# Two attention layers on one TensorE: score, value and sum matmuls as 64x64 quadrants, with part of the row sums on GpSimd

## Chip, core and metric

The kernel runs on one core of a Trainium2 chip. The metric is the time of one execution on the device, in microseconds. The core's engines are TensorE (PE in the profile; its weight loads are listed apart as PEld), VectorE (DVE), ScalarE (ACT), GpSimd (POOL) and SyncE (SP). Everything is computed in float32.

## What is computed

The reference is a chain of four attention-like layers on a tensor of 2 x 512 x 32 x 32. Layer 0 is a deformable attention with a small network for its bias, layer 1 a linear attention. Layers 2 and 3 are plain softmax attentions with 8 heads of 64 channels over 1024 positions, each with a group norm ahead of it and a residual behind it. Only those two are touched here. Cut to its core, layer 2 is (layer 3 differs in the group norm and in the order of the weights only):

```python
xn = group_norm(x)                                              # (2, 512, 1024)
q, k, v = split(einsum('oc,bcn->bon', qkv_w, xn) + qkv_b)       # 8 heads of 64 channels each
attn = softmax(einsum('bhcn,bhcm->bhnm', q, k) * 64 ** -0.5)    # over the keys m
out = einsum('bhnm,bhcm->bhcn', attn, v)
return einsum('oc,bcn->bon', proj_w, out) + proj_b + residual
```

## The kernel before

Layers 0 and 1 come first and take three quarters of the time. Then `attention` (L646) runs for layer 2 and for layer 3: it computes queries, keys and values (`queries_keys_values`, L671), branches on whether all logits are small enough to do without subtracting a maximum, runs `heads_bounded` (L783) in the branch that these inputs take, and projects the result (`project`, L423).

A query or key tile holds two heads: partitions 0 to 63 are the channels of one (par 0), 64 to 127 those of the other (par 1). `heads_bounded` goes over 16 units a layer, 32 in all: 2 batches b, 4 head pairs p, 2 halves h of 512 queries. A unit has eight blocks n of 128 keys. For each block

- `score` (L797) makes logits with the keys on the partitions: for each of the two heads a matmul with 64 rows (channels) and 128 columns (keys) over 512 queries (L804), into a PSUM tile s of 128 x 2 x 512. ACT takes the exponential into the SBUF tile e (L812), and DVE adds e to a running sum over the blocks (L816 for the first two blocks, L818 after that: seven additions a unit);
- `value` (L820) multiplies by the values: for each head a matmul with 128 rows (keys) and 64 columns (channels), accumulated over the eight blocks in a PSUM tile o of 128 x 512 (L829).

After the eighth block, a matmul with a matrix of ones, again 128 rows and 64 columns for each head (L840), adds the sum over its partitions into a PSUM tile d; DVE takes the reciprocal (L842) and multiplies o by it (L843). The result overwrites the query tile, which is no longer needed.

The order of PE's instructions is written by hand (`manual_schedule`, L847): two blocks of scores, then the two blocks of values of the step before, and so on across units. Other engines take their instructions in program order, each waiting by semaphores for its inputs and for buffers to come free. A float32 matmul shows as two records in the trace, each with a weight load of its own and one pass over the 512 columns.

[...] Here s has two buffers of two banks, o two of one bank, d two of one bank: all eight. In SBUF there are six e buffers and two each for the sum and for the reciprocal r.

Before and behind the heads: the last value projections (L739), and `project_one` (L429), which needs all four tiles of a batch, batch 0 first.

Of the kernel before, what the change touches and what calls it, by code (L numbers as in the profile page):

```python
# [11 lines left out]
F32 = mybir.dt.float32  # L12
AF = mybir.ActivationFunctionType
ALU = mybir.AluOpType
# [4 lines left out]
P = 128  # L19
# [3 lines left out]
NB = N // P  # L23
HF = 512
DH = 64
# [22 lines left out]
class Net:  # L48
# [734 lines left out]
    def heads_bounded(self, k, ones, data):  # L783

        nc = self.nc
        with ExitStack() as ctx:  # L790
            ep = self.pool(ctx, f"b{k}_e", 6)
            ap = self.pool(ctx, f"b{k}_a", 2)
            ps_s = self.pool(ctx, f"b{k}_ps_s", 2, psum=True)
            ps_o = self.pool(ctx, f"b{k}_ps_o", 2, psum=True)
            ps_d = self.pool(ctx, f"b{k}_ps_d", 2, psum=True)

            def score(unit, n):  # L797
                b, p, h, state = unit
                qs, ks, _ = data[b]
                cut = slice(h * HF, (h + 1) * HF)  # L800
                s = ps_s.tile([P, 2, HF], F32, tag="s", name=f"s{k}{b}{p}{h}{n}")
                for par in range(2):
                    rows = slice(par * DH, (par + 1) * DH)
                    nc.tensor.matmul(  # L804
                        s[:, par, :],
                        lhsT=ks[p][rows, n * P : (n + 1) * P],
                        rhs=qs[p][rows, cut],
                        start=True,
                        stop=True,
                    )  # L810
                e = ep.tile([P, 2, HF], F32, tag="e", name=f"e{k}{b}{p}{h}{n}")
                nc.scalar.activation(e, s, AF.Exp)  # L812
                state.setdefault("e", {})[n] = e
                if n == 1:
                    state["sum"] = ap.tile([P, 2, HF], F32, tag="sum", name=f"sum{k}{b}{p}{h}")
                    nc.vector.tensor_tensor(state["sum"], state["e"][0], e, ALU.add)  # L816
                elif n > 1:
                    nc.vector.tensor_tensor(state["sum"], state["sum"], e, ALU.add)  # L818

            def value(unit, n):  # L820
                b, p, h, state = unit
                v = data[b][2]
                if n == 0:
                    state["o"] = ps_o.tile([P, HF], F32, tag="o", name=f"o{k}{b}{p}{h}")
                e = state["e"].pop(n)
                for par in range(2):
                    rows = slice(par * DH, (par + 1) * DH)
                    at = (2 * p + par) * DH
                    nc.tensor.matmul(  # L829
                        state["o"][rows, :],  # L830
                        lhsT=v[:, n, at : at + DH],
                        rhs=e[:, par, :],
                        start=(n == 0),
                        stop=(n == NB - 1),
                    )
                if n == NB - 1:
                    d = ps_d.tile([P, HF], F32, tag="d", name=f"d{k}{b}{p}{h}")
                    for par in range(2):
                        rows = slice(par * DH, (par + 1) * DH)
                        nc.tensor.matmul(d[rows, :], lhsT=ones, rhs=state["sum"][:, par, :], start=True, stop=True)  # L840
                    r = ap.tile([P, HF], F32, tag="r", name=f"r{k}{b}{p}{h}")
                    nc.vector.reciprocal(r, d)  # L842
                    nc.vector.tensor_tensor(data[b][0][p][:, h * HF : (h + 1) * HF], state["o"], r, ALU.mult)  # L843

            units = [(b, p, h, {}) for b in range(B) for p in range(CT) for h in range(2)]
            steps = [(unit, n) for unit in units for n in range(NB)]
            with self.tc.manual_schedule(engines={mybir.EngineType.PE}):  # L847
                for i in range(0, len(steps) + 2, 2):
                    for unit, n in steps[i : i + 2]:
                        score(unit, n)  # L850
                    if i >= 2:
                        for unit, n in steps[i - 2 : i]:
                            value(unit, n)

    def heads_general(self, k, data):
        with ExitStack() as ctx:
# [196 lines left out]
```

## Time and profile before

| | us |
|---|---|
| median of 3 runs (4030.8 to 4035.1) | 4033.99 |
| the profiled execution, its own time | 4034.45 |
| its span in the trace | 4032.7 |
| PE busy in the span | 3924.8 (97%) |
| first score matmul of layer 2 to the start of its last d matmul | 3217.10 to 3473.77 |
| first score matmul of layer 3 | 3711.08 |

Times in the trace count from the start of the span. "Busy" of PE is the time in which at least one matmul is under way by the records; the ends of matmuls are modelled, so starts are the surer numbers. In the lists of groups a line names the source line, the engine, the operation, the tiles written and read, the shapes and the count; then the busy time in us, the mean duration of one in ns, and the idle time of the engine before such instructions with what ended it. In the view in order of time a line has start and length in us, both over a run of merged records, then engine, line, operation, tiles and count.

The DVE instructions of the heads last 1.21 us for an addition of 1024 columns, 3.36 for the reciprocal and 0.68 for the final product; an exponential on ACT lasts 1.02. POOL does nothing in the heads.

### The profile page before, as it was taken

The numbers are of one execution on the slowest core, as the hardware profiler recorded it, in microseconds if no ns is written. First come the engines' busy times: TensorE is split into PE (matmuls) and PEld (weight loads), VectorE is DVE, ScalarE is ACT, GpSimd is POOL, SyncE is SP. The second block draws the span as 40 slices with busy tenths as digits, with TensorE's granted clock in tenths as the row PEclk, the third lists the DMA queues.
The fourth block names the chain that finished last, engine by engine and source line by source line (L and its number), as shares of the span: only waits on it lengthen the run. The fifth ranks groups of instructions, "written<-read, shape, count | busy, mean of one in ns | idle before, by whom it ended". The sixth has DMA issues, their size and how long they took to land.

```text
span 4032.7 us, 34844 instructions
## 1 busy us (share of the span) xinstructions
PE 3924.8 (97%) x13792; PEld 1541.1 (38%) x13792; DVE 2264.8 (56%) x2484; ACT 1793.3 (44%) x1778; POOL 69.5 (2%) x78
## 2 busy tenths in 40 slices
PE   6999999999999999999999999999999999999999
PEld 2333333333333333333333333444464433343333
DVE  7766766766766567766766654000024277633774
ACT  5656655655655456665665553111101144211441
POOL 0000000000000000000000000000001100011000
PEclk9999999999999999999999999999999999999999
DMA  1000000000000000000000002100000000000001
GB/s 63 1 1 0 1 1 1 1 0 1 1 1 1 1 1 1 1 1 1 1 1 17 1 1 84 42 0 0 0 1 3 32 1 1 2 13 0 1 1 43
DMA packets 7521, 31.91 MB, mean 8 GB/s; under 512 B 945, under 2 KB 1457, under 8 KB 6065
## 3 DMA queue, kind: packets, MB, share of 16 engines
q1 hardware_dynamic: 6624, 27.46, 1.8%
q8 instruction: 116, 1.90, 0.2%
q10 hardware_dynamic: 720, 2.05, 0.1%
q14 instruction: 61, 0.49, 0.0%
HBM read 25.32 MB, written 4.19 MB: 7 GB/s over the span
## 4 chain that ended last, share of the span: by engine, by line
PE 91%; DVE 4%; ACT 4%; issue 0%; POOL 0%; DMA 0%; ACTq 0%; DVEq 0%
PE hp L356 41%; PE sim L325 10%; PE s L804 6%; PE o L829 6%; PE m L469 5%; PE m L478 5%; PE qk0p L698 3%; PE pb L435 3%; PE qk1p L698 3%; PE vp L739 2%; PE out_b L435 1%; DVE h L344 1%; DVE conv L203 1%; ACT h L358 1%; ACT L304 1%; ACT log L304 1%
## 5 line engine op out<-in xcount | busy, mean ns | idle before, releaser
L356 PE MATMUL hp<-h,w 128*128 128x512 f32 x4096 | 1840.3, 600 | 45.4 <-ACT h L358 34.0
L344 DVE CUSTOM_DVE_ANT_1 h<-t 128x1024 f32<-128x1024 f32 x1024 | 1249.4, 1223 | 637.0 <-PE hp L356 636.5
L358 ACT ACTIVATE h<-hp,cols 128x1024 f32<-128x1024 f32 x1024 | 1137.4, 1113 | 875.6 <-PE hp L356 870.0
L356 PEld LDWEIGHTS hp<-h,w 128*128 128x128 f32 x4096 | 750.2, 190 | 1085.2 <-issue 670.4
L325 PE MATMUL sim<-h,w 128*32 128x512 f32 x4096 | 489.7, 598 | 0.0
L812 ACT ACTIVATE e<-s 128x1024 f32<-128x1024 f32 x256 | 248.2, 1022 | 255.4 <-PE s L804 255.4
L804 PE MATMUL s<-q,k 64*128 64x512 f32 x1024 | 254.5, 615 | 5.1 <-ACT e L812 3.4
L818 DVE TENSOR_TENSOR sum<-sum,e 128x1024 f32<-128x1024 f32 x192 | 233.0, 1214 | 41.4 <-ACT e L812 30.9
L829 PE MATMUL o<-e,v 128*64 128x512 f32 x1024 | 247.5, 605 | 0.0
L325 PEld LDWEIGHTS sim<-h,w 128*32 128x32 f32 x4096 | 108.4, 109 | 343.9 <-issue 343.9
L469 PE MATMUL m<-mx,w 128*128 128x512 f32 x512 | 221.6, 594 | 0.7 <-ACT att L420 0.7
L478 PE MATMUL m<-mh,w 128*128 128x512 f32 x512 | 220.4, 592 | 0.0
L473 ACT ACTIVATE mh<-m,cols 128x512 f32<-128x512 f32 x64 | 44.0, 688 | 336.5 <-PE m L469 336.5
L486 DVE SCALAR_TENSOR_TENSOR x<-m,cols,x 128x512 f32<-128x512 f32 x16 | 12.0, 751 | 318.0 <-PE m L478 318.0
L804 PEld LDWEIGHTS s<-q,k 64*128 64x128 f32 x1024 | 88.1, 186 | 169.4 <-issue 86.9
L469 PEld LDWEIGHTS m<-mx,w 128*128 128x128 f32 x512 | 97.4, 190 | 124.3 <-issue 122.0
L478 PEld LDWEIGHTS m<-mh,w 128*128 128x128 f32 x512 | 97.3, 190 | 122.5 <-issue 122.5
L710 ACT ACTIVATE k<-qk1p,cols 128x512 f32<-128x512 f32 x32 | 22.0, 687 | 245.0 <-PE qk1p L698 245.0
L829 PEld LDWEIGHTS o<-e,v 128*64 128x64 f32 x1024 | 62.2, 136 | 169.8 <-issue 169.2
L698 PE MATMUL qk0p<-xn,qkv 128*128 128x512 f32 x256 | 118.1, 615 | 3.2 <-ACT xn L779 3.2
L435 PE MATMUL pb<-q,proj 128*128 128x512 f32 x256 | 112.2, 600 | 5.3 <-issue 5.3
L842 DVE RECIPROCAL r<-d 128x512 f32<-128x512 f32 x32 | 107.4, 3358 | 15.0 <-PE d L840 15.0
(165 smaller groups left out, 1999.9 us busy)
## 6 DMA issues: line engine op xcount, KB each, us to landing
w<-in_mlp_w SPq DMA_DIRECT2D x8, 1024.0 KB, 11.8
qkv<-in_l_qkv SPq DMA_DIRECT2D x8, 768.0 KB, 6.6
x<-in_x SPq DMA_DIRECT2D x8, 512.0 KB, 8.0
out<-x SPq DMA_DIRECT2D x8, 512.0 KB, 2.6
proj<-in_l_proj SPq DMA_DIRECT2D x8, 256.0 KB, 6.2
l1w<-in_l_w SPq DMA_DIRECT2D x1, 1280.0 KB, 5.4
ow<-in_out_w ACTq DMA_DIRECT2D x1, 1024.0 KB, 12.2
qkv<-in_l_qkv ACTq DMA_DIRECT2D x1, 768.0 KB, 8.2
```

The costliest lines, as they stand in the source:

```text
L325: nc.tensor.matmul(sim[at : at + 32, :], lhsT=self.l0w3[:, 31 - s : 63 - s], rhs=h2[jj][:, h * HF : (h + 1) * HF], start=(s == 0), stop=False,
L344: nc.vector._custom_dve(TENSOR_ADD_SAT, out=h1, in0=t[:, 0, j, :].unsqueeze(1).to_broadcast([P, H, W]), in1=t[:, 1, j, :].unsqueeze(2).to_ ...
L356: nc.tensor.matmul(hp[:, cut], lhsT=self.l0w2, rhs=flat[:, cut], start=True, stop=True)
L358: nc.scalar.activation(y, hp, AF.Relu, bias=self.col("cpb_b2"))
L435: nc.tensor.matmul(acc, lhsT=wt[:, o * P : (o + 1) * P], rhs=att[t][:, cut], start=(t == 0), stop=(t == CT - 1))
L469: nc.tensor.matmul(acc, lhsT=w1[t][:, o * P : (o + 1) * P], rhs=xn[t], start=(t == 0), stop=(t == CT - 1))
L478: nc.tensor.matmul(acc, lhsT=w2[t // 4][:, t % 4, o * P : (o + 1) * P], rhs=hs[t], start=(t == 0), stop=(t == nh - 1),)
L698: nc.tensor.matmul(acc, lhsT=qkv[c][:, at : at + P], rhs=xn[c][:, cut], start=(c == 0), stop=(c == CT - 1),)
L804: nc.tensor.matmul(s[:, par, :], lhsT=ks[p][rows, n * P : (n + 1) * P], rhs=qs[p][rows, cut], start=True, stop=True,)
L812: nc.scalar.activation(e, s, AF.Exp)
L818: nc.vector.tensor_tensor(state["sum"], state["sum"], e, ALU.add)
L829: nc.tensor.matmul(state["o"][rows, :], lhsT=v[:, n, at : at + DH], rhs=e[:, par, :], start=(n == 0), stop=(n == NB - 1),)
```

## The change

Only `heads_bounded` changes.

- Scores: each head's matmul is cut into two, of 64 keys each, so that a block has four matmuls of 64 rows and 64 columns, one in each quadrant of the array. The tile s is the same as before.
- Values: each head's matmul is cut by rows into two of 64 keys each. The two halves of the keys accumulate apart, in two banks of o (o[:, 0] and o[:, 1]), which are added at the end: ACT copies o[:, 0] to the result tile (the former query tile), and DVE adds o[:, 1] to it there.
- Sums: the matmul with ones is cut in the same way, with two banks of d. ACT copies one to t, DVE adds the other, takes the reciprocal in place and multiplies the result tile by it. This is now a function of its own, `divide`.
- The row sums: blocks 0, 1, 3 and 5 are added by GpSimd (three additions, tile some), blocks 2, 4, 6 and 7 by DVE (three additions, tile sum), and DVE adds the two (one more).
- The order on PE: one block of scores, one block of values (two blocks behind), and `divide` two blocks after the last values of its unit.
- Buffers: o and d have one buffer of two banks each instead of two of one bank; some and t (tag r) have one, sum two.

Besides what the diff shows, the built program has this order for DVE within a unit: the sum of blocks 2 and 4, the product that ends the unit before, blocks 6 and 7, the addition of some, the addition of o[:, 1], that of d[:, 1], the reciprocal. On ACT the copy of o stands between the exponentials of the next unit's blocks 1 and 2, the copy of d between those of blocks 3 and 4. The first value matmul of a unit waits for the DVE addition of o[:, 1] of the unit before. The first sum of a unit on POOL waits for the addition of some of the unit before.

```diff
+        halves = [slice(0, DH), slice(DH, P)]
...
-            ap = self.pool(ctx, f"b{k}_a", 2)
+            ap = self.pool(ctx, f"b{k}_a", 1)
+            ap2 = self.pool(ctx, f"b{k}_a2", 2)
             ps_s = self.pool(ctx, f"b{k}_ps_s", 2, psum=True)
-            ps_o = self.pool(ctx, f"b{k}_ps_o", 2, psum=True)
-            ps_d = self.pool(ctx, f"b{k}_ps_d", 2, psum=True)
+            ps_o = self.pool(ctx, f"b{k}_ps_o", 1, psum=True)
...
-                for par in range(2):
-                    rows = slice(par * DH, (par + 1) * DH)
-                    nc.tensor.matmul(
-                        s[:, par, :],
-                        lhsT=ks[p][rows, n * P : (n + 1) * P],
-                        rhs=qs[p][rows, cut],
-                        start=True,
-                        stop=True,
-                    )
+                for par, rows in enumerate(halves):
+                    for c in range(2):
+                        at = n * P + c * DH
+                        nc.tensor.matmul(
+                            s[halves[c], par, :], lhsT=ks[p][rows, at : at + DH], rhs=qs[p][rows, cut], start=True, stop=True
+                        )
...
                 if n == 1:
-                    state["sum"] = ap.tile([P, 2, HF], F32, tag="sum", name=f"sum{k}{b}{p}{h}")
-                    nc.vector.tensor_tensor(state["sum"], state["e"][0], e, ALU.add)
-                elif n > 1:
+                    state["some"] = ap.tile([P, 2, HF], F32, tag="some", name=f"some{k}{b}{p}{h}")
+                    nc.gpsimd.tensor_tensor(state["some"], es[0], e, ALU.add)
+                elif n in (3, 5):
+                    nc.gpsimd.tensor_tensor(state["some"], state["some"], e, ALU.add)
+                elif n == 4:
+                    state["sum"] = ap2.tile([P, 2, HF], F32, tag="sum", name=f"sum{k}{b}{p}{h}")
+                    nc.vector.tensor_tensor(state["sum"], es[2], e, ALU.add)
+                elif n in (6, 7):
                     nc.vector.tensor_tensor(state["sum"], state["sum"], e, ALU.add)
+                if n == NB - 1:
+                    nc.vector.tensor_tensor(state["sum"], state["sum"], state["some"], ALU.add)
...
-                    state["o"] = ps_o.tile([P, HF], F32, tag="o", name=f"o{k}{b}{p}{h}")
...
+                    state["o"] = ps_o.tile([P, 2, HF], F32, tag="o", name=f"o{k}{b}{p}{h}")
+                o, e = state["o"], state["e"][n]
+                for r, rows in enumerate(halves):
+                    for par in range(2):
+                        at = (2 * p + par) * DH
+                        nc.tensor.matmul(
+                            o[halves[par], r, :],
+                            lhsT=v[rows, n, at : at + DH],
+                            rhs=e[rows, par, :],
+                            start=(n == 0),
+                            stop=(n == NB - 1),
+                        )
                 if n == NB - 1:
...
+                    res = data[b][0][p][:, h * HF : (h + 1) * HF]
+                    nc.scalar.copy(res, o[:, 0, :])
+                    nc.vector.tensor_tensor(res, o[:, 1, :], res, ALU.add)
+
+            def divide(unit):
+                b, p, h, state = unit
+                d = ps_o.tile([P, 2, HF], F32, tag="d", name=f"d{k}{b}{p}{h}")
+                for r, rows in enumerate(halves):
                     for par in range(2):
...
+                        nc.tensor.matmul(
+                            d[halves[par], r, :], lhsT=ones[rows, :], rhs=state["sum"][rows, par, :], start=True, stop=True
+                        )
+                t = ap.tile([P, HF], F32, tag="r", name=f"r{k}{b}{p}{h}")
+                nc.scalar.copy(t, d[:, 0, :])
+                nc.vector.tensor_tensor(t, d[:, 1, :], t, ALU.add)
+                nc.vector.reciprocal(t, t)
+                res = data[b][0][p][:, h * HF : (h + 1) * HF]
+                nc.vector.tensor_tensor(res, res, t, ALU.mult)
...
-                for i in range(0, len(steps) + 2, 2):
-                    for unit, n in steps[i : i + 2]:
-                        score(unit, n)
-                    if i >= 2:
-                        for unit, n in steps[i - 2 : i]:
-                            value(unit, n)
+                for i in range(len(steps) + 4):
+                    if i < len(steps):
+                        score(*steps[i])
+                    if 2 <= i < len(steps) + 2:
+                        value(*steps[i - 2])
+                    if i >= 4 and steps[i - 4][1] == NB - 1:
+                        divide(steps[i - 4][0])
```

More of the change, by code (lines that the diff above doesn't have):

```diff
@@ L801, in score @@
                 s = ps_s.tile([P, 2, HF], F32, tag="s", name=f"s{k}{b}{p}{h}{n}")
-                for par in range(2):
-                    rows = slice(par * DH, (par + 1) * DH)
-                    nc.tensor.matmul(
-                        s[:, par, :],
-                        lhsT=ks[p][rows, n * P : (n + 1) * P],
-                        rhs=qs[p][rows, cut],
-                        start=True,
-                        stop=True,
-                    )
+                for par, rows in enumerate(halves):
[4 more added lines that the diff above has]
+                        )
                 e = ep.tile([P, 2, HF], F32, tag="e", name=f"e{k}{b}{p}{h}{n}")
                 nc.scalar.activation(e, s, AF.Exp)
-                state.setdefault("e", {})[n] = e
+                es = state.setdefault("e", {})
+                es[n] = e
                 if n == 1:
-                    state["sum"] = ap.tile([P, 2, HF], F32, tag="sum", name=f"sum{k}{b}{p}{h}")
-                    nc.vector.tensor_tensor(state["sum"], state["e"][0], e, ALU.add)
-                elif n > 1:
+                    state["some"] = ap.tile([P, 2, HF], F32, tag="some", name=f"some{k}{b}{p}{h}")
[6 more added lines that the diff above has]
+                elif n in (6, 7):
                     nc.vector.tensor_tensor(state["sum"], state["sum"], e, ALU.add)
+                if n == NB - 1:
+                    nc.vector.tensor_tensor(state["sum"], state["sum"], state["some"], ALU.add)
             def value(unit, n):
@@ L823, in value @@
                 if n == 0:
-                    state["o"] = ps_o.tile([P, HF], F32, tag="o", name=f"o{k}{b}{p}{h}")
[L825 to L835, printed above, removed]
@@ L836, in value @@
-                if n == NB - 1:
-                    d = ps_d.tile([P, HF], F32, tag="d", name=f"d{k}{b}{p}{h}")
-                    for par in range(2):
[L839 to L843, printed above, removed]
+                    state["o"] = ps_o.tile([P, 2, HF], F32, tag="o", name=f"o{k}{b}{p}{h}")
```

## The prediction

> **What bounds the kernel now.** I read the page first, then the busy times of the two stretches that the change touches, then one period of them in order of time, then single lines for durations.
>
> ```profile
> PE 3924.8 (97%) x13792; PEld 1541.1 (38%) x13792; DVE 2264.8 (56%) x2484; ACT 1793.3 (44%) x1778; POOL 69.5 (2%) x78
> ...
> PE 91%; DVE 4%; ACT 4%; issue 0%; POOL 0%; DMA 0%; ACTq 0%; DVEq 0%
> ...
> L812 ACT ACTIVATE e<-s 128x1024 f32<-128x1024 f32 x256 | 248.2, 1022 | 255.4 <-PE s L804 255.4
> L804 PE MATMUL s<-q,k 64*128 64x512 f32 x1024 | 254.5, 615 | 5.1 <-ACT e L812 3.4
> L818 DVE TENSOR_TENSOR sum<-sum,e 128x1024 f32<-128x1024 f32 x192 | 233.0, 1214 | 41.4 <-ACT e L812 30.9
> L829 PE MATMUL o<-e,v 128*64 128x512 f32 x1024 | 247.5, 605 | 0.0
> ...
> L842 DVE RECIPROCAL r<-d 128x512 f32<-128x512 f32 x32 | 107.4, 3358 | 15.0 <-PE d L840 15.0
> ```
>
> PE carries the chain. Each f32 matmul has two records (1024 records, 512 calls). ACT waits for scores; PE hardly waits for ACT. The two head stretches, by engine:
>
> ```profile
> 3217.00:3480.00 263.00, 258.40 (x1093) 80.80 (x1094) 196.95 (x144) 126.69 (x130) 0.00 (x0) 1.00 0.03 10
> 3711.00:3976.00 265.00, 260.85 (x1096) 81.87 (x1097) 196.96 (x144) 125.40 (x129) 0.00 (x0) 0.99 0.00 1
> ```
>
> Columns: length, then PE, weight loads, DVE, ACT, POOL. So PE bounds these 528 us; DVE has 25% to spare, ACT half. One period (two key blocks) in order of time, weight loads marking the starts of passes:
>
> ```profile
> 3272.60 0.30 PEld L804 LDWEIGHTS s<-q,k 64*128 64x128 f32 x4 [0.81 <-ACT e L812]
> 3272.60 1.99 PE L804 MATMUL s<-q,k 64*128 64x512 f32 x8
> 3273.14 0.19 PEld L804 LDWEIGHTS s<-q,k 64*128 64x128 f32 x2 [0.23 <-issue]
> 3273.57 0.19 PEld L804 LDWEIGHTS s<-q,k 64*128 64x128 f32 x2 [0.23 <-issue]
> ...
> 3274.52 0.20 PEld L829 LDWEIGHTS o<-e,v 128*64 128x64 f32 x4 [0.76 <-issue]
> ...
> 3275.00 0.14 PEld L829 LDWEIGHTS o<-e,v 128*64 128x64 f32 x2 [0.28 <-issue]
> 3275.43 0.14 PEld L829 LDWEIGHTS o<-e,v 128*64 128x64 f32 x2 [0.29 <-issue]
> 3276.39 0.29 PEld L804 LDWEIGHTS s<-q,k 64*128 64x128 f32 x3 [0.81 <-ACT e L812]
> ```
>
> A pass (two matmuls side by side) starts 0.43 us after the last one (3273.14 to 3273.57; 0.4293 over 27 steps of the L478 stream). Around a change of shape it is longer: 0.54 and 0.48 after the first pass, and 0.52 to 0.53 before it. The period is 3276.39 - 3272.60 = 3.79 = 8 x 0.429 + 0.35: **0.35 us per period is the price of two changes of shape.** A unit (four periods and the d passes) takes 16.00 (d starts at 3251.86 and 3267.86).
>
> **What the Trainium skill says.** (1) "TensorEngine Tiling (Array Packing)", Key Properties: changing the tiling mode, not just the tile, drains TensorE. The trace agrees: 0.35 us per two changes. (2) "TensorE: Matmul & The Clock Gate", Part 3: a weight load overlaps running matmuls only if its row group differs. The trace disagrees: full-height loads (0.19 us) in the L478 stream leave passes at 0.43. (3) "SBUF — State Buffer", Who interferes with whom: a DVE instruction with two SBUF inputs and a GpSimd instruction reading SBUF hold a port in turn; the later one blocks. No run here shows it: no such pair overlaps in the trace of before.
>
> **The change, part by part.** *Quadrants.* A block of scores becomes four 64x64 matmuls, and so do the values: still two passes of 512 columns per stage, 2 x 0.429 = 0.858 us, if four run at once. Four at once is shown for column tiles: L325's 16 records take 1.92 us a visit (4 passes plus one change), with passes 0.43 apart. All three stages have one shape now, so I cost a boundary at nothing: loads of the next stage lie under the pass before, as between consecutive score blocks. PE per unit: 17 x 0.858 = **14.59** against 16.00, 1.41 less. This is a gain on the path.
>
> *One o buffer.* o was double; now the next unit's first value matmul waits until o is emptied by an ACT copy and then a DVE add. Let the last value stage start at 0. Its second pass starts at 0.43 and, with a row's 0.59, ends at 1.02. ACT took up the exponential of the preceding score block at 0.21 and, at the 0.92 spacing of back-to-back ones, is free at 1.13. The copy takes 0.58 (L195, 128x512), to 1.71; the add 0.68 (L843's form), from 1.75 to 2.43. PE has one score block to do meanwhile, to 1.72, and then waits. Behind the waiting matmul stand all later scores, so ACT starves too. It restarts at 2.48, and its first pass is 0.10 longer, as after the start-up wait at 3220.76. **Stall 0.77 + 0.10 = 0.87 per boundary.**
>
> *DVE and POOL.* DVE's order is: sum of blocks 2 and 4, the previous unit's product, blocks 6 and 7, the POOL part, the o add, the d add, reciprocal. From o add to o add there is a loop: two value stages and a score stage (2.67 with the longer first pass), d (1.02), copy and add with waits (0.06 + 0.58 + 0.06 + 0.68), reciprocal 3.38, then 1.08 + 0.60 + 1.33 + 1.33 + 1.08 for the adds and product at their observed spacings (a dependent add starts 0.10 after the last), and the o add with its wait, 0.74: 14.6. PE's unit of 14.59 + 0.87 = 15.46 hides that, with 0.9 to spare. POOL's three sums run at blocks 1, 3, 5.
>
> ```profile
> L712 POOL TENSOR_TENSOR sq<-q x16: 1894/1895/1897, 3055.6 to 3674.9; 128x1024 f32<-128x1024 f32 x16
> ```
>
> This is 1.89 us with one tile as both inputs. For two tiles (4) "GPSIMD Engine Reference", 3.1, gives 4497 ns at 2048 elements: an estimate of 2.25 at 1024. The third sum starts when block 5's exponential ends, about a microsecond before DVE wants to start its first two-input add; if the port is held it delays that add by 0.9 (1.89) to 1.25 (2.25). Of this 0 to 0.35 comes through to PE; bound below at 0, since the port can't speed DVE. I take 0.08: stall **0.95**. The e buffers, six of them, come free in time: block 2's is freed by DVE's first add, at the latest at 1.75 - 5.42 + 1.23 = -2.44 (5.42 is the loop's five steps before the o add), and the next unit's block 0 needs it at -1.51. s, sum, some and r are free long before.
>
> *ACT.* Two copies of 0.58 a unit on top of eight exponentials: 8.5 of 15.5, hidden except for the o copy above.
>
> *Start and end.* At the start the third score block waits for the first exponential and its table load as now (3220.76 - 3217.10 = 3.66). At the end d waits for two adds after block 7's and DVE's backlog, about 2.4 us, where nothing is left to fill PE. The reciprocal and product after it (about 1.5 later than now) lie under batch 0's projection.
>
> *Sum for a layer*, first score to last d: 3.66 + 269 stages x 0.8586 (230.96) + 15 boundaries x 0.95 (14.25) + 2.4 = 251.3; before 3473.77 - 3217.10 = 256.7. Saved 5.4, over two layers 10.8. PE idles longer at the end; after layer 3's heads the first four passes of L435 ran at half speed (3.4 instead of 1.7 us), and I add one more such restart, 1.7. Profiled 4034.45 - 10.8 + 1.7 = **4025**; the median, 4033.99, is 0.5 lower, which I leave aside.
>
> **The rivals.** *A, as summed: 4025*, and between 4021 (port never held, stall 0.87, a layer 250.1) and 4029. *B, the port is held and POOL's sums take 2.25 or more*: DVE's loop, 14.6 + 1.25, becomes the bound at 15.8 a unit, a layer takes 255.7, and the end is 4034.45 - 2.0 + 1.7 = 4034, no change. For it: the skill's two pages; against it: the 1.89 of L712. *C, slower: stages of quadrants don't overlap at their boundaries.* Place: each of 17 boundaries a unit, twice as many as changes of shape now, for single blocks alternate. Price: the 0.10 before the first pass now seen at a change. PE's unit is then 16.29, the stall shrinks to 0.74, 17.03 in all, a layer 274.0: 4034.45 + 2 x 17.3 = 4069. It decides above 0.03 us a boundary, where the unit passes 16.00. For it: the skill's sentence (2), and L419, the one 64x64 place, has 0.48 between its passes, though just after a change. Against it: 0.43 in three other shapes. *D, the four quadrants run only two at a time*: each stage 1.72, a unit near 30, 4034 + 32 x 14 = 4480. L325 speaks against it. *E, the boundary costs half*: o's copy starts before the exponential ends, 15.0 a unit: 4034 - 24 + 1.7 = 4012; nothing speaks for ACT going out of order.
>
> **How the numbers follow.** Chances: A 0.53, B 0.20, C 0.18, D 0.04, E 0.05. A difference under 0.2% (8 us) can't be told from none here, so faster means under 4026, slower over 4042. A lies about 0.6 below 4026: 0.32, with E 0.05: faster 0.37. Slower: C mostly (0.15), D, and a B with POOL beyond 2.5 (0.09): 0.28. The rest, 0.35, is no change. For eight in ten I go from 4017 (E and the best of A left out) to 4062 (D and the upper half of C left out). The likeliest case alone is 4021 to 4029.
>
> **What would show it.** Right: passes of four records 0.43 apart through all stages, no longer spacing at score-to-value boundaries, one idle stretch of about 0.8 us per unit at the first value matmul of a unit, released by the DVE add, and none elsewhere; a unit near 15.5. B: DVE's first sum starting when POOL's third ends, and o's add late. C: 0.5 us or more at each boundary. D: two records per 0.43. Wrong: POOL sums over 2.5 us, or waits of PE on exponentials inside a unit.

## The result, and the profile after

The changed kernel takes 4039.44 us (median of 4 runs, 4038.7 to 4040.24) against 4034.55 (median of 4, 4030.8 to 4036.28): a ratio of 1.0013, interval 0.9996 to 1.0031. That can't be told from no change. The execution that was profiled took 4040.04 us with a span of 4038.2 us, against 4034.45 and 4032.7 before.

The busy times, the engines' shares of the chain that ended last, and the groups of the heads, from the page of the changed kernel:

```profile
PE 3891.0 (96%) x15968; PEld 1545.8 (38%) x15968; DVE 2233.2 (55%) x2452; ACT 1843.3 (46%) x1842; POOL 296.3 (7%) x174
...
PE 82%; DVE 12%; ACT 4%; issue 1%; POOL 0%; DMA 0%; DVEq 0%; ACTq 0%
...
L810 ACT ACTIVATE e<-s 128x1024 f32<-128x1024 f32 x256 | 262.3, 1026 | 189.2 <-PE s L806 189.2
L835 PE MATMUL o<-e,v 64*64 64x512 f32 x2048 | 266.6, 592 | 33.9 <-DVE q L845 33.9
L806 PE MATMUL s<-q,k 64*64 64x512 f32 x2048 | 265.6, 589 | 5.1 <-ACT e L810 3.4
L817 POOL TENSOR_TENSOR some<-some,e 128x1024 f32<-128x1024 f32 x64 | 151.4, 2366 | 102.9 <-ACT e L810 102.9
```

PE is busy 34 us less, and yet the kernel isn't faster: the value matmuls now idle 33.9 us for the DVE addition of o[:, 1], and DVE's share of the chain goes from 4% to 12%. GpSimd's sum takes 2.37 us, more than both ends I had given it. The two head stretches by engine (columns as in the prediction; the second window is 14 us longer than the one shown of before, and takes in some of the projection behind the heads):

```profile
3217.00:3480.00 263.00, 238.37 (x2178) 81.55 (x2176) 178.51 (x128) 149.54 (x161) 113.45 (x48) 1.00 0.03 13
3711.00:3990.00 279.00, 254.46 (x2210) 88.39 (x2209) 184.43 (x133) 149.55 (x161) 113.39 (x48) 0.99 0.01 3
```

In the same 263 us of layer 2, PE is busy 238.4 us instead of 258.4; neither DVE (178.5) nor GpSimd (113.5) looks like a bound. That is only an average: the order of time shows what bounds. One unit, from one o addition (L845) to the next, all engines in order of time, with the stages in the middle left out:

```profile
3251.91 1.23 DVE L824 TENSOR_TENSOR sum<-sum,some 128x1024 f32<-128x1024 f32 x1
3251.99 0.58 ACT L844 COPY q<-o 128x512 f32<-128x512 f32 x1
3253.05 0.68 DVE L845 TENSOR_TENSOR q<-o,q 128x512 f32<-128x512 f32 x1
...
3253.79 1.09 PE L835 MATMUL o<-e,v 64*64 64x512 f32 x8 [1.16 <-DVE q L845]
3254.70 1.04 PE L806 MATMUL s<-q,k 64*64 64x512 f32 x8
3255.56 1.04 PE L835 MATMUL o<-e,v 64*64 64x512 f32 x8
3256.41 1.04 PE L852 MATMUL d<-sum,ones 64*64 64x512 f32 x8
3257.27 1.04 PE L806 MATMUL s<-q,k 64*64 64x512 f32 x8
3257.55 0.59 ACT L856 COPY r<-d 128x512 f32<-128x512 f32 x1 [0.66 <-PE d L852]
...
3258.89 3.35 DVE L858 RECIPROCAL r<-r 128x512 f32<-128x512 f32 x1
...
3261.26 2.36 POOL L817 TENSOR_TENSOR some<-some,e 128x1024 f32<-128x1024 f32 x1 [1.87 <-ACT e L810]
...
3262.16 2.55 DVE L820 TENSOR_TENSOR sum<-e,e 128x1024 f32<-128x1024 f32 x1
...
3267.88 1.23 DVE L824 TENSOR_TENSOR sum<-sum,some 128x1024 f32<-128x1024 f32 x1
3267.97 0.58 ACT L844 COPY q<-o 128x512 f32<-128x512 f32 x1
3269.02 0.68 DVE L845 TENSOR_TENSOR q<-o,q 128x512 f32<-128x512 f32 x1
```

Three things are to be seen.

- Stages of scores, values and sums follow each other every 0.858 us (3254.70, 3255.56, 3256.41, 3257.27). The boundaries cost nothing: PE needs the 14.59 us a unit that was forecast.
- From o addition to o addition is 3269.02 - 3253.05 = 15.97 us, and this is the unit of the whole layer (15.96 to 16.02, against 16.00 before). In it ACT has the copy of o ready at 3252.57 and 3268.55, but the DVE addition that needs it starts 0.48 and 0.47 later, when DVE comes free of L824. PE waits for DVE, and DVE isn't waiting for ACT.
- DVE's first sum of the unit (L820) starts at 3262.16, and takes 2.55 us instead of the 1.21 of an addition of this shape before. GpSimd's third sum ends at 3261.26 + 2.36 = 3263.62; L820 ends 1.09 after that. Over all units:

```profile
L820 DVE TENSOR_TENSOR sum<-e,e x32: 1800/2574/2627, 3228.0 to 3966.0; 128x1024 f32<-128x1024 f32 x32
```

The columns are shortest, median and longest in ns. So DVE is held back by some 1.35 us in each unit; the profile shows this as a longer instruction and not as an idle time.

The last d of layer 2 and the start of the projection, on PE alone:

```profile
3471.06 2.75 PE L835 MATMUL o<-e,v 64*64 64x512 f32 x24
3476.95 1.09 PE L852 MATMUL d<-sum,ones 64*64 64x512 f32 x8 [3.14 <-DVE sum L824]
```

**Where the 5.5 us of the span lie.** Layer 2's heads start 1.5 later (3218.63, before 3217.10) after work that the change doesn't touch, which is no effect of it that I can name; the kernel before differs by up to 5.5 us from run to run. From the first score to the last d a layer takes 258.3 us (3218.63 to 3476.95; 3714.77 to 3973.07), before 256.67: +1.65 in each of the two. Between the layers' heads +0.5, after the last +0.2. The sum is 1.5 + 1.65 + 0.5 + 1.65 + 0.2 = 5.5.

### The profile page after: what moved, and what is told of

Read it like the earlier page. It is cut to its first block, busy times and chain, and to the rows that moved or that the text cites. A ratio compares the mean times of both kernels' runs of the same rounds, so it can differ in the third digit from the quotient of the medians.

```text
span 4038.2 us, 39353 instructions
## 1 busy us (share of the span) xinstructions
PE 3891.0 (96%) x15968; PEld 1545.8 (38%) x15968; DVE 2233.2 (55%) x2452; ACT 1843.3 (46%) x1842; POOL 296.3 (7%) x174
## 4 chain that ended last, share of the span: by engine, by line
PE 82%; DVE 12%; ACT 4%; issue 1%; POOL 0%; DMA 0%; DVEq 0%; ACTq 0%
PE hp L356 41%; PE sim L325 10%; PE m L469 5%; PE m L478 5%; PE qk0p L698 3%; PE pb L435 3%; PE qk1p L698 3%; DVE r L858 2%; PE vp L739 2%; DVE sum L820 2%; DVE sum L822 2%; PE o L835 2%; PE out_b L435 1%; DVE h L344 1%; PE s L806 1%
## 5 line engine op out<-in xcount | busy, mean ns | idle before, releaser
L810 ACT ACTIVATE e<-s 128x1024 f32<-128x1024 f32 x256 | 262.3, 1026 | 189.2 <-PE s L806 189.2
L835 PE MATMUL o<-e,v 64*64 64x512 f32 x2048 | 266.6, 592 | 33.9 <-DVE q L845 33.9
L806 PE MATMUL s<-q,k 64*64 64x512 f32 x2048 | 265.6, 589 | 5.1 <-ACT e L810 3.4
L817 POOL TENSOR_TENSOR some<-some,e 128x1024 f32<-128x1024 f32 x64 | 151.4, 2366 | 102.9 <-ACT e L810 102.9
L835 PEld LDWEIGHTS o<-e,v 64*64 64x64 f32 x2048 | 75.4, 133 | 185.2 <-issue 124.1
L806 PEld LDWEIGHTS s<-q,k 64*64 64x64 f32 x2048 | 78.1, 133 | 147.6 <-issue 142.4
```

The source lines that it names most:

```text
L806: nc.tensor.matmul(s[halves[c], par, :], lhsT=ks[p][rows, at : at + DH], rhs=qs[p][rows, cut], start=True, stop=True)
L817: nc.gpsimd.tensor_tensor(state["some"], state["some"], e, ALU.add)
L835: nc.tensor.matmul(o[halves[par], r, :], lhsT=v[rows, n, at : at + DH], rhs=e[rows, par, :], start=(n == 0), stop=(n == NB - 1),)
```

## The experiments

The theory after this result: PE gained the 1.41 us a unit that the quadrants were to bring, and lost 1.38 to the wait for the one o buffer. The wait is that long because DVE's loop from o addition to o addition is the bound (rival B): 14.6 us of its own, and 1.35 by which GpSimd's third sum holds up L820. (By that loop I mean all that lies between two o additions: two value stages, a score stage and the d matmuls on PE, ACT's copies, and DVE's own instructions.) The rivals to it: the o buffer's wait is long for PE's or ACT's own reasons, whatever GpSimd does; or the quadrants have a hidden price. Ratios are against the kernel before, whose runs lie beside them on the same chip (medians of 4033.93 and 4035.69 us).

**1. GpSimd adds the first blocks.** The same three sums on GpSimd, but of blocks 0 to 3, so that it is done before DVE starts its own.

```diff
-                elif n in (3, 5):
+                elif n in (2, 3):
                     nc.gpsimd.tensor_tensor(state["some"], state["some"], e, ALU.add)
-                elif n == 4:
+                elif n == 5:
...
-                    nc.vector.tensor_tensor(state["sum"], es[2], e, ALU.add)
+                    nc.vector.tensor_tensor(state["sum"], es[4], e, ALU.add)
```

> The changed kernel, but GpSimd adds blocks 0, 1, 2, 3 and VectorE 4, 5, 6, 7: the same three and four additions, only GpSimd is done earlier. Theory (VectorE's loop from o addition to o addition bounds a unit, and the hold-up of its first sum by GpSimd's third, 2.57 instead of 1.2 us, is in that loop): the first sum takes 1.2 us, the loop falls under PE's own 14.59 + 0.87, a unit takes 15.5 instead of 15.97, a layer's heads about 250 instead of 259, the whole 4022. Rival (GpSimd's additions are merely slow, or VectorE's work as such is the bound): the same additions, so 4039 as before.

Measured: 4024.85 us, ratio 0.9974 (0.9965 to 0.9984), 15.51 to 15.54 a unit but for the last of a layer. The unit is as expected, the whole 2.9 more. L820 in this kernel:

```profile
L820 DVE TENSOR_TENSOR sum<-e,e x32: 1215/1218/1927, 3229.0 to 3952.6; 128x1024 f32<-128x1024 f32 x32
```

And a boundary, in order of time:

```profile
3251.28 0.58 ACT L844 COPY q<-o 128x512 f32<-128x512 f32 x1
3251.89 0.69 DVE L845 TENSOR_TENSOR q<-o,q 128x512 f32<-128x512 f32 x1 [0.52 <-ACT q L844]
3252.64 1.09 PE L835 MATMUL o<-e,v 64*64 64x512 f32 x8 [0.71 <-DVE q L845]
```

L820 is back at 1.22 us, DVE now waits for ACT's copy, and PE idles 0.71 a unit. The same additions on the same engines, placed so that the two don't meet, give 0.45 us a unit: with the hold-up gone, DVE no longer bounds the unit. One more thing differs: DVE's product for the unit before (L860, at 3245.56) now comes ahead of L820 (3246.17) and not behind it. Experiment 8 shortens the hold-up and leaves DVE's order as it was. What is left is the wait for PE's and ACT's part, 15.52 - 14.59 = 0.93; the prediction had 0.87 for it, and 0.95 with its allowance for the hold-up.

**2. All seven sums on DVE.**

```diff
                 if n == 1:
-                    state["some"] = ap.tile([P, 2, HF], F32, tag="some", name=f"some{k}{b}{p}{h}")
-                    nc.gpsimd.tensor_tensor(state["some"], es[0], e, ALU.add)
...
+                    nc.vector.tensor_tensor(state["sum"], es[0], e, ALU.add)
+                elif n > 1:
                     nc.vector.tensor_tensor(state["sum"], state["sum"], e, ALU.add)
-                if n == NB - 1:
-                    nc.vector.tensor_tensor(state["sum"], state["sum"], state["some"], ALU.add)
```

> The changed kernel with all seven row sums on VectorE, none on GpSimd. Theory: no hold-up, but the o addition now stands behind the next unit's first sum in VectorE's queue, which waits for an exponential; o comes free about 0.6 later than PE alone would have it, a unit takes about 16.1, the whole 4040. Rival (the loss is GpSimd's alone): without it a unit takes 15.5 and the whole 4022.

Measured: 4043.13 us, ratio 1.0022 (1.0013 to 1.0031), 16.13 a unit. No GpSimd, no hold-up, and the unit is 0.16 longer than with them. A boundary, and DVE's longest wait in the unit after it:

```profile
3253.93 0.58 ACT L837 COPY q<-o 128x512 f32<-128x512 f32 x1
3254.06 1.22 DVE L815 TENSOR_TENSOR sum<-e,e 128x1024 f32<-128x1024 f32 x1 [0.36 <-ACT e L810]
3255.21 0.68 DVE L838 TENSOR_TENSOR q<-o,q 128x512 f32<-128x512 f32 x1
3255.94 0.66 PE L828 MATMUL o<-e,v 64*64 64x512 f32 x4 [1.31 <-DVE q L838]
...
3259.01 1.23 DVE L817 TENSOR_TENSOR sum<-sum,e 128x1024 f32<-128x1024 f32 x1 [1.99 <-ACT e L810]
```

The o addition stands behind the first sum of the next unit, which itself has to wait for its exponential. DVE is idle for 0.36 and 1.99 us here, so what bounds is not the amount of its work (experiment 5 fits the same work into 14.59) but the order: o comes free 0.61 later in the unit than in experiment 1 (16.13 against 15.52), where 0.6 was expected.

**3. Two buffers for o.** If PE doesn't wait for o, DVE's loop is open. There are banks for a second o if d takes its place among the buffers of s.

```diff
-            ps_o = self.pool(ctx, f"b{k}_ps_o", 1, psum=True)
+            ps_o = self.pool(ctx, f"b{k}_ps_o", 2, psum=True)
...
-                d = ps_o.tile([P, 2, HF], F32, tag="d", name=f"d{k}{b}{p}{h}")
+                d = ps_s.tile([P, 2, HF], F32, tag="s", name=f"d{k}{b}{p}{h}")
```

> The changed kernel with two buffers of o (four banks); d takes its two banks from the rotation of s. GpSimd's and VectorE's work is unchanged. Theory (o's one buffer is what ties PE to VectorE): no idle PE at unit boundaries, 14.6 a unit (17 stages of 0.8586) although VectorE's first sum may still be held up, the heads about 238 a layer, the whole 3999. Rival (VectorE with its hold-ups is the bound by its throughput): a unit stays near 16.0 and the whole at 4039. A third possibility: d in the rotation of s delays the scores behind it until d is emptied; then PE idles there instead and a unit is 15 or more.

Measured: 3999.35 us, ratio 0.9913 (0.9898 to 0.9928), 14.59 a unit, 238.0 us from the first score to the last d. L820 stays as slow as in the changed kernel:

```profile
L820 DVE TENSOR_TENSOR sum<-e,e x32: 1804/2576/2628, 3226.1 to 3924.6; 128x1024 f32<-128x1024 f32 x32
```

A boundary of this kernel, on PE and DVE:

```profile
3249.61 1.04 PE L835 MATMUL o<-e,v 64*64 64x512 f32 x8
3250.20 0.68 DVE L845 TENSOR_TENSOR q<-o,q 128x512 f32<-128x512 f32 x1
3250.47 1.04 PE L806 MATMUL s<-q,k 64*64 64x512 f32 x8
...
3254.68 0.24 PEld L806 LDWEIGHTS s<-q,k 64*64 64x64 f32 x8 [0.62 <-DVE r L857]
3254.76 1.04 PE L806 MATMUL s<-q,k 64*64 64x512 f32 x8
```

The next unit's values start at 3249.61, before the addition of the last o at 3250.20. The same hold-up of 1.35 us is there and costs nothing, because no matmul waits for DVE within the unit. What d's new place costs is in the last two lines: a score's weight load waits 0.62 for the DVE addition that empties d, and its matmuls start 0.08 us after that load. They still start on time, 0.86 after the stage before (3253.90), but this margin is narrow. From the first score of a layer on PE waits only for the first exponential (1.7 us) and for the last d (3.2), so 14.59 is the price of the quadrants as such.

**4. The kernel before, with single blocks alternating.** The changed order of PE without quadrants: shapes change twice as often.

```diff
-                for i in range(0, len(steps) + 2, 2):
-                    for unit, n in steps[i : i + 2]:
-                        score(unit, n)
+                for i in range(len(steps) + 2):
+                    if i < len(steps):
+                        score(*steps[i])
                     if i >= 2:
-                        for unit, n in steps[i - 2 : i]:
-                            value(unit, n)
+                        value(*steps[i - 2])
```

> The kernel before with its own shapes, but single blocks of scores and values alternating as in the changed kernel: 16 changes of shape a unit instead of 8. Theory (0.35 us per two changes, 0.18 each): a unit takes 16.00 + 8 x 0.18 = 17.4, the whole 4034 + 32 x 1.41 = 4080. Rival (the gaps at the boundaries are waits for exponentials or buffers, not the change of shape): 4034, or a different amount.

Measured: 4080.42 us, ratio 1.0112 (1.0096 to 1.0127), 17.40 a unit. PE, in order of time:

```profile
3250.81 1.08 PE L829 MATMUL o<-e,v 128*64 128x512 f32 x4
3251.82 1.13 PE L804 MATMUL s<-q,k 64*128 64x512 f32 x4
3252.88 1.08 PE L829 MATMUL o<-e,v 128*64 128x512 f32 x4
```

Stages start 1.01 and 1.06 us apart instead of 0.858. The waits of this trace name no exponential and no buffer for PE's matmuls at these boundaries. Eight more changes of shape a unit cost 17.40 - 16.00 = 1.40, 0.175 each; with quadrants in the same order of blocks a unit takes 14.59 (experiment 3), which is 16 x 0.176 = 2.81 less. The price of a change of shape holds, and one shape for all stages removes all of it.

**5. Both: two o buffers, and all sums on DVE.** (The edits of 2 and 3.)

> Two buffers of o (d in the rotation of s), and all seven row sums on VectorE. Theory (with o double, VectorE has a whole unit of slack, and its 14.4 us of work a unit still fit into PE's 14.6): 14.6 a unit as with GpSimd's help, the whole 3998; the last d waits less than with GpSimd, for the hold-up is gone. Rival (GpSimd's part is needed, VectorE would be the bound without it): more than 15 a unit, the whole over 4010.

Measured: 3997.8 us, ratio 0.9912 (0.9898 to 0.9926), 14.59 a unit. The layer's stretch, by engine:

```profile
3218.00:3460.00 242.00, 235.79 (x2178) 83.10 (x2179) 215.07 (x175) 150.69 (x162) 0.00 (x0) 0.99 0.03 12
```

DVE is busy 215 of 242 us and holds nothing up; GpSimd isn't needed. What cost 0.2% over the kernel before with one o buffer (experiment 2) is free with two.

**6. ACT copies both halves of o.** One o buffer, but the wait for it is taken off DVE: both banks are emptied by ACT, and DVE adds later.

```diff
                     nc.scalar.copy(res, o[:, 0, :])
-                    nc.vector.tensor_tensor(res, o[:, 1, :], res, ALU.add)
+                    other = ap.tile([P, HF], F32, tag="other", name=f"other{k}{b}{p}{h}")
+                    nc.scalar.copy(other, o[:, 1, :])
+                    nc.vector.tensor_tensor(res, other, res, ALU.add)
```

> The changed kernel, one buffer of o, but ScalarE copies both halves of o, the second into an SBUF tile of its own, and VectorE adds the two there: o no longer waits for VectorE's queue. Theory: the loop through VectorE is open, although its first sum is still held up to 2.5 us; PE waits only for the two copies, 14.59 + about 0.65, so 15.25 a unit, the whole 4018. Rival (what makes PE wait is that o is single, whoever empties it): about as the changed kernel or its first-blocks variant, 15.5 to 16.0 a unit, 4025 to 4039.

Measured: 4020.02 us, ratio 0.9968 (0.9956 to 0.998), 15.29 a unit on average. Who PE waited for (us in all, times, the longest in us), and the first GpSimd sum of a unit:

```profile
PE o L835 <- ACT other L846: 14.0, 30, 0.5
```

```profile
L815 POOL TENSOR_TENSOR some<-e,e x32: 2354/2712/2745, 3222.3 to 3936.6; 128x1024 f32<-128x1024 f32 x32
```

L820 is still 2.57 here, and the unit is 0.68 shorter than in the changed kernel: with DVE no longer between o and PE its hold-up costs nothing. I had not expected the second line. DVE's addition for o now has two tiles of SBUF as inputs instead of one of PSUM, and GpSimd's sum, which starts while it runs, goes from 2.36 to 2.71 us, while the addition itself keeps its 0.69: the hold-up works the other way round as well.

**7. Two o buffers, and GpSimd on the first blocks.** (The edits of 1 and 3.)

> Two buffers of o, and GpSimd adds blocks 0 to 3. Theory: 14.6 a unit as with two buffers alone; only the last d of a layer is reached about 1 us earlier (3.2 instead of 4.3 after the last values), so the whole is 3997, at most 2 less than with two buffers alone. Rival (the hold-up still costs PE something with two buffers): more than 5 us less.

Measured: 3997.93 us, ratio 0.9913 (0.99 to 0.9927), 14.59 a unit. Experiments 3, 5 and 7 can't be told apart: with two o buffers it makes no difference which of these three ways the sums are added, though without the hold-up the last d waits 2.2 us instead of 3.2. They are the fastest versions I have, 0.9% under the kernel before.

**8. GpSimd reads one tile twice.** Is GpSimd's 2.36 instead of the 1.89 of L712 a matter of its inputs, or of the other engines? The GpSimd sums take the same tile as both inputs. This leaves block 0 out of the row sums and doesn't accumulate on GpSimd.

```diff
-                    nc.gpsimd.tensor_tensor(state["some"], es[0], e, ALU.add)
+                    nc.gpsimd.tensor_tensor(state["some"], e, e, ALU.add)
                 elif n in (3, 5):
-                    nc.gpsimd.tensor_tensor(state["some"], state["some"], e, ALU.add)
+                    nc.gpsimd.tensor_tensor(state["some"], e, e, ALU.add)
```

> The changed kernel, but each of GpSimd's three additions takes one tile as both inputs, so the row sums leave out block 0 and do not accumulate on GpSimd. Theory (an addition of two different tiles takes 2.36 us on GpSimd, one tile twice 1.89 as in the kernel before; the end of the third sets when VectorE starts): GpSimd's additions take 1.9, VectorE's first sum 2.1, a unit 15.55, the whole 4026. Rival (2.36 comes from contention in the heads and not from the second tile): still 2.36, 15.97 and 4039.

Measured: 4026.26 us, ratio 0.998 (0.9973 to 0.9988), 15.51 to 15.56 a unit. GpSimd's later sums and L820, over all units and in one of them:

```profile
L817 POOL TENSOR_TENSOR some<-e x64: 1892/1892/1896, 3226.2 to 3952.0; 128x1024 f32<-128x1024 f32 x64
L820 DVE TENSOR_TENSOR sum<-e,e x32: 1336/2100/2152, 3227.9 to 3952.8; 128x1024 f32<-128x1024 f32 x32
...
3260.70 1.89 POOL L817 TENSOR_TENSOR some<-e 128x1024 f32<-128x1024 f32 x1 [2.34 <-ACT e L810]
3261.60 2.07 DVE L820 TENSOR_TENSOR sum<-e,e 128x1024 f32<-128x1024 f32 x1
```

With one tile GpSimd takes 1.89 in the heads too: the second tile costs 0.47. And L820 becomes 0.47 shorter with it, 2.10 instead of 2.57: the hold-up ends with the GpSimd sum. L820 ends 1.08 after it here (3263.67 against 3262.59), where it was 1.09 in the changed kernel. The hold-up of 2.10 - 1.22 = 0.88 that is left fits into DVE's slack of 0.9, and the unit is that of experiment 1: this is the kernel that the prediction's 1.89 would have given, and it lands at 4026.

## Where the prediction was right and where it failed

The time fell within the range, and "no change" had been given 0.35, but the likeliest case (A, 4025) and the likeliest outcome (faster, 0.37) didn't happen. The range held 4039 because it was drawn to take in B and half of C; it says nothing for A, whose own range ended at 4029. What happened is B, 5 us slower than B's 4034.

- **Quadrants: right.** Four at once, 0.858 a stage, boundaries at nothing, 14.59 a unit. C (a drain at each boundary) and D (two at a time) didn't happen; experiment 3 shows the gain alone, 1.41 a unit. The Trainium skill, "TensorEngine Tiling (Array Packing)", Key Properties, says that changing the tiling mode drains TensorE; the trace agrees that a change costs time, and experiment 4 prices it: 0.175 us.
- **One o buffer, 0.87 a boundary: right as PE's and ACT's part of it.** Experiments 1 and 8 have 0.92 to 0.97 in all. In experiment 1 PE restarts 2.61 after the start of its last value stage (3250.03 to 3252.64) instead of 2.48, for ACT takes up the exponential ahead of the copy at 0.33 (3250.36) and not at 0.21. Experiment 6, where a second ACT copy (0.58) takes the place of DVE's part, has 0.70.
- **DVE's loop of 14.6: right.** With the 1.35 of the hold-up it gives 15.95, measured 15.97.
- **The hold-up: this is the step that failed.** "Of this 0 to 0.35 comes through to PE; [...] I take 0.08: stall **0.95**." Measured: the third sum holds DVE 1.35, of which 15.97 - 14.59 - 0.87 = 0.51 comes through (0.45 by experiment 1, which has 0.93 left without it). The term was mis-sized in two places. GpSimd's sum with two tiles takes 2.36, outside both ends of 1.89 and 2.25. The second was the estimate from the Trainium skill, "GPSIMD Engine Reference", 3.1, halved for half the elements, and it was the nearer one; the first was an instruction of one tile and no measure for this. I weighed them as equals, and took a value at the lower end. The mechanism was in the Trainium skill, "SBUF — State Buffer", Who interferes with whom: a DVE instruction with two SBUF inputs and a GpSimd instruction that reads SBUF keep each other out. The trace agrees: L820 ends 1.09 after GpSimd's sum, in experiment 8 1.08. With GpSimd's price of 2.25 the loop would already have been 15.85, over PE's 15.46, and the forecast B. B was on record with 0.20; its signs, "DVE's first sum starting when POOL's third ends, and o's add late", are both seen, except that the record of L820 starts before GpSimd's end and contains the wait.
- **The last d: 2.4 forecast, 3.3 measured** (the next stage could start at 3471.06 + 3 x 0.858 = 3473.63, d starts at 3476.95; 3.14 idle by records), since DVE comes to the end with the hold-up behind it: in experiment 1, without the hold-up, it is 2.3 (3463.96 + 2.57 = 3466.53 to 3468.80).
- **One more half-speed restart, 1.7:** layer 2's projection takes 56.88 us from first to last record instead of 55.53, 1.35 more; layer 3's 56.35 instead of 56.27. Layer 2's first passes start 0.85 us apart now, before 0.43. About right, and by its side other work between the layers became 1.5 shorter.
- **Two of the recorded sums are off by their own terms.** A's lower end of 4021 leaves the restart out (4034.45 - 13.2 + 1.7 is 4023), and C's layer comes to about 275 and not 274.0. Neither bears on what happened.

From forecast to result: a layer was to take 251.3 and takes 258.3. Of the 7.0, 14 boundaries x (1.38 - 0.95) are 6.0 (the first boundary has 0.71 of idle time, since GpSimd's hold-up hasn't filled DVE's slack by then), the end 0.9; 0.1 is left. Two layers are 14.0; the other places add 2.2 (1.5 + 0.5 + 0.2), and the restart is already counted among these, so its 1.7 comes off: 4025 + 14.0 + 2.2 - 1.7 = 4039.5, and the profiled execution took 4040.04.

So where did the gain go? PE's 1.41 a unit turned into a wait at one place, because the banks that the quadrants' halves need were taken from o's second buffer. By experiment 1, 0.45 of it is GpSimd's hold-up; the other 0.93 is the single buffer alone, and with two buffers both vanish (experiment 3). Not tried: shortening the wait of the last d.

## What to carry to other kernels

When an accumulator loses its second buffer, every engine that empties it comes into one loop with TensorE: add up that whole loop, with every instruction that stands between two emptyings on that engine, and compare it with TensorE's period, because a slack of 0.9 us in 15.5 can be eaten by a single hold-up, here of 1.35. Price work that goes to GpSimd by a row with the same inputs, and place it where VectorE isn't about to start an instruction with two SBUF inputs, or see that nothing waits for VectorE there. Before giving a buffer up, look whether a short-lived tile can share another one's ring: here that made the difference between no gain and 0.9%.

## What the runs showed of the hardware

- A VectorE addition with two SBUF inputs that is held up by a GpSimd sum shows no idle time before it: the wait is in its recorded duration, 2.57 us instead of 1.22. It works both ways (GpSimd 2.36 to 2.71 in experiment 6). Additions with one PSUM input (0.68) and the reciprocal (3.35) beside a GpSimd sum kept their durations.
- GpSimd's addition of 128x1024 f32 takes 2.36 us with two tiles and 1.89 with the same tile twice, with VectorE and ScalarE busy beside it in both.
- Four 64x64 matmuls of 512 f32 columns run together, in 0.858 us a stage, and stages that accumulate, that don't, and that use other weights follow each other with no loss; each change between the shapes 64x128 and 128x64 costs 0.175 us (experiment 4).
